# Placing a tile's weighted sum next to another tile's scores, and sharing a division between VectorE and GpSimd, in a cross-attention and expert kernel

## The chip, the cores and the metric

The kernel runs on one core of one Trainium2 chip. The metric is the device time in microseconds of one execution; lower is better. Three executions of the kernel before took 1203.09, 1205.06 and 1205.17 us, a median of 1205.06 us.

## What is computed

The input `x` has 32 sequences of 256 tokens with 256 features. Two layers follow each other, each with a residual and a scalar gate:

```python
x = x + tanh(g_xattn) * attention(layernorm(x), ctx, ctx)   # 16 heads, 77 keys, then @ W.T + b
x = x + tanh(g_ffn) * ffn(layernorm(x))

def attention(q, k, v):          # 16 heads of 16 features
    scores = q @ k.T / sqrt(16)
    scores = where(causal or padded, -inf, scores)
    return softmax(scores) @ v @ W.T + b

def ffn(x):                      # 2 groups of 4 experts, 2 experts per token
    shared = swiglu(x @ w_in.T) @ w_out.T
    h = swiglu(x @ w1.T)
    group = argmax(softmax(x @ wg.T + gb))
    p = softmax(x @ we.T + eb over the group's experts) * p_group
    a, b = the two largest of p
    return shared + p[a] * h @ w2[a].T + p[b] * h @ w2[b].T
```

Everything is float32.

## The kernel before

The 8192 tokens are cut into 16 blocks of 512, a block into 4 tiles of 128 tokens (t = 0 to 3); a tile fills the 128 partitions. Three things go on at once for different blocks.

The attention of a tile is a chain of small steps, each a function:

- `first_stats`, `normed`, `queries`: the layer norm of `x` on VectorE, and its transposition on TensorE (tile `pt`, copied by ScalarE into `qT`). `biased` adds the output bias to `x` on GpSimd (L338).
- `scores` (L353): 8 small matmuls, each over 32 rows of TensorE, into the PSUM tile `sc` of four banks. Its pool `ps_sc` has one buffer.
- `masked` (L366): VectorE adds the mask and moves the scores to SBUF (`ws`, two buffers in turn). `largest` (L378, L379): the maximum of each head and its scaling.
- `exps` (L387): ScalarE, one instruction for each head, with its sum. In block 0 half of the heads go another way: `shifted` (L396) on VectorE, `wide` (L410) on ScalarE, `summed` (L415) on VectorE.
- `divided` (L424, L425): VectorE takes the reciprocal of the sums and multiplies all 16 heads of 77 values in place.
- `transposed` (L440): ten transpositions into three banks `ptr`, which ScalarE copies into `aT` (L443).
- `weighted` (L465): the sum of values, small matmuls that each write 32 columns, into `vT`; ScalarE copies it into `oT`.
- `o_proj` (L485), `residual` (L502), `stats2`, `normed2`, `keep`: the output matmul `po`, the residual, the second layer norm and its transposition into `xT` (copied at L302).

The dense work of a block follows: `shared` (matmuls `ph`, L790, and `pys`, L842), `routed` (`pr`, L818), and the experts' matmuls `py` (L905) for 128 tokens of one pair of experts at a time. Those tokens are collected through DRAM: `rec` is written to `rows` by an indirect DMA from GpSimd (L859), and read back as `r_q` by SyncE's queue; `hp` (L898) transposes it, and GpSimd writes `out` (L925). Which pair a token takes is worked out by `logits` (`plT`), `choice`, `places` and `listing` on VectorE, in many short instructions.

The order is written out by hand. The dense work is a generator that pauses twice in each unit (after a unit's matmuls, and after their eviction); every other step has a place, counted in such units, and is issued when the counter reaches it. A block from number 5 on takes 28 units. The places stand in the table `PLACES`: one row for a step, whose first four numbers are for the tiles of block 0, the next four for blocks 1 to 4, the ninth for blocks 5 to 14, and the tenth for block 15. A tile's place is `s0 + t * gap` and the step's number on top; steps on TensorE come half a unit later. The engines then run their queues strictly in the order in which the steps were issued. All PSUM tiles but `sc` share one pool of four banks.

In blocks 5 to 14 `gap` is 7, `scores` is at -2 and `weighted` at 9.5. So `weighted` of a tile comes 2.5 units before `scores` of the tile two behind it, which are at -2 + 14.

Of the kernel before, what the change touches and what calls it, by code (L numbers as in the profile page):

```python
# [11 lines left out]
ALU = mybir.AluOpType  # L12
AX = mybir.AxisListType

P = 128
D = 256
NC_ = D // P
NH = 16
# [15 lines left out]
BB = 2  # L34
EPS = 1e-5
WIDE = 8
SURE = 22
AHEAD = 4
MASKED = -1.0e30
# [2 lines left out]
PLACES = {  # L42


    "s0": (12.5, 17, 20, 12.5, 17, 17, 18, 16, 16.5, 16.5),
    "gap": (3, 14.5, 3, 3.5, 3, 5, 4, 5.5, 7, 7),
    "stats": (-8, -8, -16, -13.5, -12, -11, -10.5, -9, -8.5, -9),
    "stats_gap": (0.25, 0, -3, -4.25, 0.75, 1.25, 1.25, 1.5, 0.75, 1),
    "bias": (-0.5, -1, -5.5, -8.5, -6, -1.5, -0.5, -1.5, -2.5, -2.5),
    "normed": (-4.5, -3, -5, -3, -3.5, -4.5, -3.5, -4, -4, -5),  # L50
    "normed_gap": (4, 2.75, 1.5, 3.75, 1, 2, 3.25, 1.75, 1.5, 1.75),
    "queries": (-2.5, -3, -5.5, -3.5, -4, -3, -3.5, -4, -3, -4.5),
    "queries_copy": (0, 0.5, -0.5, 3, 0.5, 0.75, 0, 0.75, 0, 1.75),
    "scores": (-2.5, -5, -1.5, -1, -2, -1, -1, 0, -2, -1.5),
    "masked": (0.5, -1.5, -0.5, 0.5, 0.5, 0, 0, 1, 1, 1),
    "largest": (1, 1, 2, 1, 2, 2, 1, 1.5, 2.5, 2.5),
    "exps": (3.5, 4.5, 5.5, 4.5, 3, 3, 2, 3, 3.5, 3),
    "exps_gap": (-1, -1.25, -0.75, -1.5, 0.5, 0.5, 0.5, 0.5, 0.75, 0.5),
    "divided": (5.2, 5.2, 6.2, 5.2, 5.7, 5.2, 4.2, 5.2, 6.7, 6.7),
    "transposed": (8.5, 8, 8, 7.75, 8, 6, 7.5, 7, 8.5, 8.5),  # L60
    "aT": (0.75, 0.5, 1.75, 0.75, 0.25, 0.25, 0, 0.25, 0.5, 0.25),
    "weighted": (9.5, 9.5, 10.5, 9.5, 10, 9, 8, 10, 9.5, 9.5),
    "oT": (0.25, 1.5, 0, 1, 0, 0.75, 1, 0, 0, 0),
    "o_proj": (12, 11, 12.5, 11, 10.5, 10.5, 10, 11, 10, 10),
    "residual": (13, 13, 13.5, 12.5, 11.5, 12, 11, 12, 11, 11),
    "stats2": (13.5, 13.5, 14.5, 13, 12.5, 13.5, 12.5, 13, 12, 12),
    "normed2": (16, 15, 15, 14.5, 14, 14.5, 13.5, 14, 13.5, 13),
    "keep": (16, 15.5, 15.5, 15.5, 14.5, 14.5, 16, 15, 14, 14),
    "xT": (1.25, 1.25, 2.25, 1, 0.25, 0.75, 0, 0, 0.5, 0.5),
    "logits": (10, 12, 15.5, 14.5, -1, -1, 0, -1, -1, -1),  # L70
    "lT": (0, -0.5, -1.25, -2.5, 0.25, 0, 0, 0, 0.25, 0),
    "choice": (11, 10.5, 17, 18.5, 0, 0, 0, -0.5, -0.5, -0.5),
    "choice1": (14, 9.5, 12, 15.5, 1, 1, 1, 0.5, 0.5, 1),
    "choice2": (12.5, 14.5, 10.5, 10.5, 7.5, 2.5, 1.5, 1, 1, 2),
    "choice3": (15.5, 13, 17.5, 14.5, 2, 8.5, 9.5, 2.5, 2.5, 4.5),
    "places": (15.5, 14, 20, 18.5, 3, 3.5, 3, 2, 2.5, 3),
    "places1": (16, 11.5, 11, 3, 4.5, 7, 4, 3.5, 8, 3.5),
    "places2": (16, 17.5, 24, 24.5, 9.5, 5.5, 8.5, 8.5, 4, 7.5),
    "listing": (5, 2, 0, 2.5, 19.5, 9.5, 7.5, 7, 5.5, 5),
    "listing_gap": (2.25, 5, 1.25, 3.75, 1.75, 2, 3, 4.25, 4.75, 4),  # L80
    "load": (-0.5, 2, -2, 0, -10, 9, 4.5, 6, 19.5, 6.5),
    "biased": (-2.5, -2.5, 0, 5, 7.5, 3.5, 5.5, 4.5, 3.5, 11),
    "biased_gap": (2.25, 2.25, 1.5, 2, 0.375, 1.25, 1.75, 2.75, 0.5, 1.25),
    "ends": (9.5, 13.5, 6.5, 11, 5, 10, 7, -3, 11, 6),
    "ends_gap": (2.5, 2, 0, -0.5, 2.25, -2.5, -1, 4.25, 0, 1.75),
    "context": (2, 5, 4, 6.5, -8, 4, -5.5, 0.5, 5.5, 5),
    "shifted": (2, 2, 3, 3.5, -2.5, -1.5, 4.5, -1.5, -5, -13),
    "wide": (4.6, 3.6, 4.1, 4.1, 4, 1.5, 0.5, -0.5, 9, 6),
    "summed": (4.9, 4.9, 4.4, 4.4, -1, 1, -2.5, -9, 5, 0.5),
}  # L90


# [1 line left out]
def kernel(  # L94
# [19 lines left out]
    nc = tc.nc  # L114
    NBLK, SK = mask.shape[0], mask.shape[2]
# [259 lines left out]
    def largest(s, t):  # L375
        i = s["i"]
        mx = p2.tile([P, NH], F32, tag="mx", name=f"mx_{i}_{t}")
        nc.vector.tensor_reduce(mx, s["ws", t], AX.X, ALU.max)  # L378
        nc.vector.tensor_scalar_mul(mx, mx, -(DH**-0.5))  # L379
        s["mx", t] = mx  # L380
        s["pr", t] = p2.tile([P, NH, SK], F32, tag="pr", name=f"pr_{i}_{t}")
        s["rc", t] = p2.tile([P, NH], F32, tag="rc", name=f"rc_{i}_{t}")
# [11 lines left out]
    def shifted(s, t):  # L394
        heads = slice(NH - WIDE, NH)
        nc.vector.scalar_tensor_tensor(  # L396
            s["pr", t][:, heads, :],
            s["mx", t][:, heads].unsqueeze(2).to_broadcast([P, WIDE, SK]),
            DH**0.5,
            s["ws", t][:, heads, :SK],  # L400
            ALU.mult,
            ALU.add,
        )
        s["exps", t] = s.get(("exps", t), 0) + WIDE
        s["shifted", t] = True

    def wide(s, t):
        assert s.pop(("shifted", t))
        pr = s["pr", t][:, NH - WIDE :, :]
        nc.scalar.activation(pr, pr, AF.Exp, scale=DH**-0.5)  # L410
        s["wide", t] = True

    def summed(s, t):
        assert s.pop(("wide", t))
        nc.vector.tensor_reduce(  # L415
            s["rc", t][:, NH - WIDE :], s["pr", t][:, NH - WIDE :, :], AX.X, ALU.add
        )
        s["summed", t] = True

    def divided(s, t):  # L420
        assert s["i"] or s.pop(("summed", t))
        pr, rc = s["pr", t], s.pop(("rc", t))
        assert s.pop(("exps", t)) == NH
        nc.vector.reciprocal(rc, rc)  # L424
        nc.vector.tensor_tensor(  # L425
            pr, pr, rc.unsqueeze(2).to_broadcast([P, NH, SK]), ALU.mult
        )

    def transposed(s, t):

# [554 lines left out]
    def at(place, fn, pe=False):  # L985
        events.append((place + 0.5 * pe, len(events), fn))
# [7 lines left out]
    def place(b, what, t=0):  # L994
        return PLACES[what][t if b == 0 else 3 + min(b, 5) + (b + 1 == NBLK)]

    def tile_events(b, t, e):
        def p(what):
            return e + place(b, what, t)
# [3 lines left out]
        at(p("largest"), lambda: largest(blocks[b], t))  # L1003
        for k in range(4 - 4 * WIDE // NH if b == 0 else 4):
            at(
# [3 lines left out]
        if b == 0:  # L1009
            at(p("shifted"), lambda: shifted(blocks[b], t))  # L1010
            at(p("wide"), lambda: wide(blocks[b], t))
            at(p("summed"), lambda: summed(blocks[b], t))
        at(p("divided"), lambda: divided(blocks[b], t))
        at(p("transposed"), lambda: transposed(blocks[b], t), pe=True)
        for k in range(3):
# [41 lines left out]
    for b in range(NBLK):  # L1057
        e = begins[b]
        gap = place(b, "gap")
        s0 = e - place(b, "s0") - (NT - 1) * gap  # L1060
# [39 lines left out]
    def finish(tiles):  # L1100
        gens = [pair_tile(k) for k in tiles]
        for g in gens[:AHEAD]:
            next(g)
        for g in gens[:2]:
            next(g)
            next(g)
        for _ in pair_tiles(gens):
            pass

    with tc.manual_schedule(  # L1110
# [16 lines left out]
        count = nc.values_load(counts[0], min_val=0, max_val=n_rest)  # L1127
        finish(rest[:SURE])
        with tc.If(count > SURE):
            finish(rest[SURE:])  # L1130

# [76 lines left out]
```

## Time and profile before

| What | us |
|---|---|
| median of three executions | 1205.06 |
| the profiled execution, whole | 1204.88 |
| its span, first to last instruction | 1203.1 |
| TensorE busy with matmuls | 1158.4 |
| VectorE busy | 898.4 |
| ScalarE busy | 615.1 |
| GpSimd busy | 291.6 |

The profile names the engines PE (TensorE's matmuls), PEld (its weight loads), DVE (VectorE), ACT (ScalarE), POOL (GpSimd) and SP (SyncE, which issues DMAs). A group's row gives the line, the engine, the operation, what is written from what, the sizes, the number of instructions and their busy and mean time. A row of the timeline gives the start in us from the span's start, the length in us, and the same names; a bracket at its end gives the idle time before it and what ended it. Matmuls on TensorE overlap, so the time of a group is best read from its start to the start of the next.

### The profile page before, as it was taken

To read this page: it belongs to the slowest core of one execution; us is meant where nothing else is said; L and a number is where in the kernel's file an instruction comes from. 1 tells how busy PE (TensorE), PEld (TensorE's weight loads), DVE (VectorE), ACT (ScalarE), POOL (GpSimd) and SP (SyncE) were. 2 spreads that over 40 slices of the span, in tenths; PEclk is the share of its full clock that TensorE was granted. 3 is DMA by queue.
4 is the path that set the end of the run, shared out by engine and by line. 5 is a ranking of instruction groups with operands and counts; after the bars stand their busy time and mean duration, and the time that the engine had idled before them with its cause. 6 is when DMAs were issued, how large, how long until landed. Compare 5 with 4: busy or idle time off the path is not lost.

```text
span 1203.1 us, 23398 instructions
## 1 busy us (share of the span) xinstructions
PE 1158.4 (96%) x7548; PEld 785.0 (65%) x7548; DVE 898.4 (75%) x2504; ACT 615.1 (51%) x2594; POOL 291.6 (24%) x509
## 2 busy tenths in 40 slices
PE   4799999999999999999999999999999999999997
PEld 3576555556575766767576676757667575757886
DVE  7988979897868688786868878686887868574222
ACT  3875675555555645555564555556455555411110
POOL 2013131222130312313031231302223122224222
PEclk9899999999999999999999999999999999999999
DMA  7102061213131121313112131311213020134442
GB/s 251 40 15 93 15 245 37 71 41 124 40 106 58 67 85 65 112 41 107 58 67 84 58 120 40 102 62 67 84 53 107 28 81 31 46 102 165 126 116 78
DMA packets 39016, 98.89 MB, mean 82 GB/s; under 512 B 6824, under 2 KB 17962, under 8 KB 38384
## 3 DMA queue, kind: packets, MB, share of 16 engines
q1 hardware_dynamic: 28976, 60.78, 16.5%
q0 software_dynamic: 9488, 36.47, 7.7%
q8 instruction: 64, 1.05, 0.4%
q14 instruction: 56, 0.46, 0.1%
q10 hardware_dynamic: 432, 0.13, 0.0%
HBM read 60.50 MB, written 39.74 MB: 83 GB/s over the span
## 4 chain that ended last, share of the span: by engine, by line
PE 69%; issue 6%; POOL 2%; ACT 2%; DVE 1%; POOLq 0%; DVEq 0%; ACTq 0%
PE pr L818 15%; PE py_q L905 15%; PE ph L790 14%; PE pys L842 7%; PE vT L465 4%; PE po L485 3%; PE ptr L440 3%; PE sc L353 3%; POOL out L925 2%; PE pt L299 2%; PE hp_q L898 2%; ACT hT_q L900 1%; PE plT L529 1%; ACT sa L802 1%; ACT aT L443 0%
## 5 line engine op out<-in xcount | busy, mean ns | idle before, releaser
L387 ACT ACTIVATE pr<-ws,mx 128x77 f32<-128x77 f32 x992 | 341.3, 349 | 10.5 <-DVE mx L379 10.0
L790 PE MATMUL ph<-xT,win_sb 128*128 128x512 f32 (+1 forms) x544 | 242.4, 581 | 1.8 <-ACT xT L302 1.0
L818 PE MATMUL pr<-w_sb,xT 128*128 128x512 f32 x512 | 243.1, 603 | 0.7 <-DVE rec L833 0.3
L905 PE MATMUL py_q<-w_sb,hT_q 128*128 x784 | 184.8, 382 | 4.3 <-ACT hT_q L900 4.3
L387 ACT ACTIVATION_READ_ACCUMULATOR pr<-ws,mx 128x1 f32 x992 | 188.9, 190 | 0.0
L905 PEld LDWEIGHTS py_q<-w_sb,hT_q 128*128 128x128 f32 x784 | 143.5, 190 | 25.7 <-ACT hT_q L900 7.4
L790 PEld LDWEIGHTS ph<-xT,win_sb 128*128 128x128 f32 x544 | 97.6, 191 | 87.3 <-issue 72.9
L818 PEld LDWEIGHTS pr<-w_sb,xT 128*128 128x128 f32 x512 | 90.5, 190 | 84.9 <-issue 74.1
L285 POOL TENSOR_TENSOR rs_f<-ve_f,nhalf 128x1 f32<-128x1 f32 x64 | 36.7, 573 | 380.3 <-DVE ve_f L283 356.4
L443 ACT COPY aT<-ptr 124x512 f32<-124x512 f32 (+1 forms) x192 | 86.8, 523 | 71.0 <-PE ptr L440 70.8
L842 PE MATMUL pys<-wout_sb,gT 128*128 128x256 f32 x512 | 121.7, 380 | 0.0
L859 POOL DMA_INDIRECT rows<-rec,posi x64 | 69.2, 1081 | 204.0 <-DVE rec L856 85.6
L842 PEld LDWEIGHTS pys<-wout_sb,gT 128*128 128x128 f32 x512 | 95.6, 190 | 26.0 <-issue 12.6
L925 POOL DMA_INDIRECT out<-acc_q,r_q x49 | 61.5, 1255 | 146.8 <-DVE acc_q L916 120.8
L425 DVE TENSOR_TENSOR pr<-pr,rc 128x1232 f32<-128x1232 f32 x64 | 92.9, 1452 | 2.2
L366 DVE TENSOR_TENSOR ws<-sc,mb 128x1232 f32<-128x1232 f32 x64 | 91.6, 1432 | 2.0 <-PE sc L353 2.0
L378 DVE TENSOR_REDUCE mx<-ws 128x16 f32<-128x1248 f32 x64 | 92.5, 1445 | 0.5
L440 PE MATMUL ptr<-ident,pr 128*124 128x128 f32 x640 | 83.6, 277 | 2.9 <-DVE sr L832 1.1
L440 PEld LDWEIGHTS ptr<-ident,pr 128*124 128x124 f32 x640 | 73.2, 141 | 19.2 <-issue 6.2
L302 ACT COPY xT<-pt 128x256 f32<-128x256 f32 x64 | 23.8, 371 | 116.8 <-PE pt L299 116.8
L905 PE MATMUL py_last<-w_sb,hT_last 128*128 x352 | 79.6, 379 | 0.3 <-ACT hT_last L900 0.3
L828 ACT ACTIVATE sr<-pr 128x512 f32<-128x512 f32 x64 | 38.0, 593 | 78.1 <-PE pr L818 63.6
(181 smaller groups left out, 1577.8 us busy)
## 6 DMA issues: line engine op xcount, KB each, us to landing
r_q<-rows SPq DMA_DIRECT2D x49, 386.0 KB
va<-in_vd SPq DMA_DIRECT2D x16, 640.0 KB
r_last<-rows SPq DMA_DIRECT2D x22, 386.0 KB
x<-in_x SPq DMA_DIRECT2D x64, 128.0 KB
kbd<-in_kbd SPq DMA_DIRECT2D x16, 308.0 KB
w_sb<-in_w2T SPq DMA_DIRECT2D x4, 1024.0 KB
mi<-in_mask SPq DMA_DIRECT2D x16, 77.0 KB
win_sb<-in_w_inT SPq DMA_DIRECT2D x1, 1024.0 KB
```

The lines of the kernel that those rows point to most:

```text
L366: nc.vector.tensor_tensor(ws[:, :, :SK].rearrange("p (g h) k -> p g h k", g=RG), s.pop(("sc", t))[:, :, : NC_ * PK].rearrange("p g (h k) - ...
L378: nc.vector.tensor_reduce(mx, s["ws", t], AX.X, ALU.max)
L387: nc.scalar.activation(s["pr", t][:, h, :], s["ws", t][:, h, :SK], AF.Exp, bias=s["mx", t][:, h : h + 1], scale=DH**-0.5, accum_out=s["rc" ...
L425: nc.vector.tensor_tensor(pr, pr, rc.unsqueeze(2).to_broadcast([P, NH, SK]), ALU.mult)
L440: nc.tensor.transpose(pt[:CR, (r - r0) * P : (r - r0 + 1) * P], pr[:, row : row + CR], ident)
L443: s["aTc", t, r0 // 4] = lambda r0=r0, n=n, pt=pt: nc.scalar.copy(aT[:, r0 : r0 + n, :].rearrange("k r q -> k (r q)"), pt[:CR, : n * P])
L790: nc.tensor.matmul(ab[half][:, : n * P], lhsT=win_sb[:, c, f0 : f0 + P], rhs=s["xT"][:, c, cols], start=(c == 0), stop=(c == NC_ - 1),)
L818: nc.tensor.matmul(ab[half], lhsT=s["xT"][:, c, t * P : (t + 1) * P], rhs=w1_sb[:, c, half * HID : (half + 1) * HID], start=(c == 0), stop ...
L842: nc.tensor.matmul(py[:, :D], lhsT=s["g"][:, m, t * P : (t + 1) * P], rhs=wout_sb[:, m, :], start=(m == 0), stop=(m == NM - 1),)
L859: put(nc.gpsimd.indirect_dma_start(out=rows, out_offset=bass.IndirectOffsetOnAxis(ap=s["pos"][:, t, :], axis=0), in_=rec, in_offset=None,), i)
L905: nc.tensor.matmul(py[:, j * D : (j + 1) * D], lhsT=hT[:, m, :], rhs=w2_sb[:, m, bass.ds(e_at[j], D)], start=(m == 0), stop=(m == NM - 1),)
L925: done_with(nc.gpsimd.indirect_dma_start(out=out, out_offset=bass.IndirectOffsetOnAxis(ap=ids, axis=0), in_=acc, in_offset=None, bounds_ch ...
```

## The change

Three things are changed.

First, in blocks 5 to 14 the places of `scores` go from -2 to -4.5. With a gap of 7, `scores` of tile t + 2 then comes at 9.5, where `weighted` of tile t stands too, directly ahead of it. In block 15 `scores` goes to -2 and `weighted` stays at 9.5, with the same gap of 7.

Second, the other places are set anew, in all blocks. In blocks 5 to 14 `masked` goes from 1 to 2 and `largest` from 2.5 to 2, `o_proj` from 10 to 11.5 and `residual` from 11 to 12; the loads of `x` come 5 units earlier. In block 0 the second `queries` come ahead of the second `scores`.

Third, in blocks 0 and 1 (`SHARED = 2`) the multiplication of `divided` is split: heads 0 to 7 on VectorE, heads 8 to 15 on GpSimd.

```diff
+SHARED = 2
...
-    "s0": (12.5, 17, 20, 12.5, 17, 17, 18, 16, 16.5, 16.5),
-    "gap": (3, 14.5, 3, 3.5, 3, 5, 4, 5.5, 7, 7),
+    "s0": (12.5, 14, 21, 14.5, 17, 17, 18, 16, 16.5, 16.5),
+    "gap": (3, 4, 3, 2, 3, 5, 4, 5.5, 7, 7),
...
-    "scores": (-2.5, -5, -1.5, -1, -2, -1, -1, 0, -2, -1.5),
-    "masked": (0.5, -1.5, -0.5, 0.5, 0.5, 0, 0, 1, 1, 1),
-    "largest": (1, 1, 2, 1, 2, 2, 1, 1.5, 2.5, 2.5),
-    "exps": (3.5, 4.5, 5.5, 4.5, 3, 3, 2, 3, 3.5, 3),
+    "scores": (-2.5, -2.5, -1.5, 0, -2.5, -1.5, -1.5, 0, -4.5, -2),
+    "masked": (1, -1.5, -1, 0.5, 0.5, 0, 0, 1, 2, 2),
+    "largest": (1, 1.5, 2, 1.5, 2, 2, 1, 1.5, 2, 2.5),
+    "exps": (3.5, 4.5, 5.5, 4.5, 3, 3, 2, 3, 4, 4),
...
-    "weighted": (9.5, 9.5, 10.5, 9.5, 10, 9, 8, 10, 9.5, 9.5),
+    "weighted": (9, 9, 10, 9, 10, 9, 8.5, 9.5, 9.5, 9.5),
...
-    "o_proj": (12, 11, 12.5, 11, 10.5, 10.5, 10, 11, 10, 10),
-    "residual": (13, 13, 13.5, 12.5, 11.5, 12, 11, 12, 11, 11),
+    "o_proj": (12, 11, 11.5, 10.5, 11, 10.5, 10, 11, 11.5, 10),
+    "residual": (13, 13, 13.5, 12, 11.5, 12, 11, 12, 12, 11),
...
-    "load": (-0.5, 2, -2, 0, -10, 9, 4.5, 6, 19.5, 6.5),
+    "load": (4, 11.5, -1.5, -2, -0.5, 18.5, 17, 8, 24.5, 7),
...
         nc.vector.reciprocal(rc, rc)
-        nc.vector.tensor_tensor(
-            pr, pr, rc.unsqueeze(2).to_broadcast([P, NH, SK]), ALU.mult
-        )
+
+        parts_ = [(nc.vector, 0, NH)]
+        if s["i"] < SHARED:
+            parts_ = [(nc.vector, 0, NH // 2), (nc.gpsimd, NH // 2, NH)]
+        for engine, h0, h1 in parts_:
+            engine.tensor_tensor(
+                pr[:, h0:h1], pr[:, h0:h1],
+                rc[:, h0:h1].unsqueeze(2).to_broadcast([P, h1 - h0, SK]), ALU.mult,
+            )
```

## The prediction

> **What bounds the kernel now.** I read the page's busy shares first, then its slices, then busy time by stage, then TensorE's waits in the stage where it idles.
>
> ```profile
> PE 1158.4 (96%) x7548; PEld 785.0 (65%) x7548; DVE 898.4 (75%) x2504; ACT 615.1 (51%) x2594; POOL 291.6 (24%) x509
> PE   4799999999999999999999999999999999999997
> ```
>
> TensorE is busy for 96% of the span and below nine tenths only in the first two slices and the last. The stages (start:end, span, then busy time of PE, PEld, DVE, ACT, POOL, granted clock, DMA share, GB/s) make that sharper:
>
> ```profile
> 10.00:50.00 40.00, 25.02 (x304) 18.82 (x296) 38.97 (x72) 25.21 (x107) 4.12 (x6) 0.96 0.45 147
> 50.00:60.00 10.00, 7.71 (x39) 5.71 (x40) 7.78 (x18) 8.83 (x50) 0.87 (x3) 0.83 0.32 111
> 300.00:1050.00 750.00, 746.38 (x4895) 498.38 (x4895) 586.00 (x1641) 409.40 (x1738) 177.37 (x309) 1.00 0.21 71
> ```
>
> From 300 to 1050 us TensorE has 3.6 us of holes: there only a shorter TensorE stream shortens the kernel. From 10 to 50 us VectorE is busy 38.97 of 40 us and TensorE waits for it:
>
> ```profile
> PE sc L353 <- DVE ws L366: 10.0, 3, 7.0
> PE pt L299 <- DVE xn L290: 7.2, 1, 7.2
> PE pt L299 <- ACT aT L443: 3.7, 1, 3.7
> ```
>
> (waiter, what it waited for, us in all, times, longest.) So the change has two separate parts: the middle is TensorE's stream, the start VectorE's queue.
>
> **Part 1: `weighted` next to `scores`.** TensorE's timeline, one tile of the steady middle:
>
> ```profile
> 603.26 1.98 PE L818 MATMUL pr<-w_sb,xT 128*128 128x512 f32 x4
> 605.17 1.08 PE L465 MATMUL vT<-aT,va 124*32 124x128 f32 x32
> 606.18 1.98 PE L818 MATMUL pr<-w_sb,xT 128*128 128x512 f32 x4
> 608.00 1.03 PE L485 MATMUL po<-wo_sb,oT 128*128 128x256 f32 x4
> ...
> 611.03 1.88 PE L818 MATMUL pr<-w_sb,xT 128*128 128x512 f32 x4
> 612.84 0.81 PE L353 MATMUL sc<-kbd,qT 32*128 32x154 f32 x16
> 613.58 0.66 PE L299 MATMUL pt<-ident,xn 128*128 128x128 f32 x4
> 614.07 1.88 PE L818 MATMUL pr<-w_sb,xT 128*128 128x512 f32 x4
> 615.79 1.89 PE L842 MATMUL pys<-wout_sb,gT 128*128 128x256 f32 x8
> ```
>
> Read start to start, since matmuls overlap. Four pr matmuls between full-array neighbours take 615.79 - 614.07 = 1.72. Before `sc` they take 612.84 - 611.03 = 1.81: entering a small-tile group costs 0.09. After `vT` they take 608.00 - 606.18 = 1.82: leaving costs 0.10 (0.06 when transposes follow: four pt take 0.49 after `sc`, 0.44 else, in the same view). Before `vT` they take 1.91. `vT` itself takes 1.01, `sc` 0.74.
>
> A rule speaks against a gain: the Trainium skill, "TensorEngine Tiling (Array Packing)", Key Properties, says that changing the tiling mode, not merely the tile, drains TensorE. `vT` tiles columns (124*32) and `sc` rows (32*128), so side by side they still change mode. The trace of before has such a pair:
>
> ```profile
> 259.54 1.08 PE L465 MATMUL vT<-aT,va 124*32 124x128 f32 x32
> 260.55 0.81 PE L353 MATMUL sc<-kbd,qT 32*128 32x154 f32 x16
> 261.28 0.66 PE L299 MATMUL pt<-ident,xn 128*128 128x128 f32 x4
> ```
>
> `vT` 1.01, `sc` 0.73: nothing is added between them. By the row a pairing saves one entry and one exit, by the rule only about one of them. I take the row.
>
> Count from the built order of TensorE's instructions: runs of small-tile groups (`sc`, `vT`, `plT`) fall from 135 to 98; 40 `sc` stand directly behind a `vT`, against 5. Pricing every boundary of both orders by the class it falls in (entry 0.09 from a full group, 0.19 from ph or pr into `vT`, 0 from transposes; exit 0.10, or 0.06 into transposes) gives 24.7 us before and 17.8 after: **-6.9 us**. By the rule it would be about -3.4. The matmuls are otherwise the same in number and shape.
>
> Does a new wait eat it? `ps_sc` has one buffer, so `scores` of tile t+1 must wait for `masked` of t. Before, `masked` ends 7.9 to 11.8 us ahead of the next `sc` in steady blocks. After, `masked` stands later, `scores` earlier. The tightest case (t = 1): VectorE after the last py of the block does the two acc (0.48 each), then ws (1.43), about 2.5 us with 0.15 to wake; TensorE has plT 0.58, ptr 1.15, ph 1.72, pl 0.20, vT 1.01 = 4.66 before `sc`. Slack 2.1 us. For t = 2 the orders match before's, where ws ends at 658.24 and vT at 659.88: 1.6. A second tight place is `pt` of tile 0's `normed2`: its VectorE queue starts 0.6 us later than before (acc and `masked` now precede `largest`), where before had 653.69 - 652.75 = 0.9 in hand; 0.1 to 0.3 is left after part 1 shortens TensorE. Nothing is lost if these hold; I allow 0 to 0.3 us per block, up to 3 us in all, as width.
>
> `o_proj` and `residual` move later by 1.5 and 1 steps; `keep` stays, with 5 us of full-array matmuls between po and pt to hide residual 0.48, statistics 0.6 + 0.15, pow 0.57 and xn 0.41. On SP, the load of x now stands ahead of the block's first `r_q` load, not behind its last: it waits for an x freed some 8 steps earlier, and `r_q` is used twelve units (over 20 us) later. No cost.
>
> **Part 2: the halves of the division in blocks 0 and 1.** VectorE saves half of 1.44, 0.72, in each of 8 tiles, if GpSimd's half runs beside it. The trace speaks against that:
>
> ```profile
> 214.41 1.45 DVE L425 TENSOR_TENSOR pr<-pr,rc 128x1232 f32<-128x1232 f32 x1
> 214.43 2.01 POOL L338 TENSOR_TENSOR x<-x,bo 128x256 f32<-128x256 f32 x1
> ...
> 156.16 0.74 POOL L338 TENSOR_TENSOR x<-x,bo 128x256 f32<-128x256 f32 x1
> 156.41 1.79 DVE L425 TENSOR_TENSOR pr<-pr,rc 128x1232 f32<-128x1232 f32 x1
> ```
>
> An addition of 0.72 alone takes 2.01 behind a division, and a division of 1.44 takes 1.79 behind an addition: whoever comes second waits until the first is done. "SBUF — State Buffer", Who interferes with whom, says the same and for which: VectorE with two SBUF inputs or in a two-port mode excludes GpSimd's reads. VectorE's half comes first (it waits for nothing), GpSimd's follows; then VectorE's next instruction counts. In block 0 that is `shifted` (mx and ws, both SBUF) for tiles 0 to 2 and `normed2` for tile 3 (a TENSOR_SCALAR; one like it took 0.90 for 0.41 beside GpSimd): all blocked until GpSimd ends. No row has 128x616 on GpSimd; from 0.72 at 256, scaled fully, 1.73; with 0.2 fixed (its 2-element copy), 1.45. I take 1.6.
>
> So a tile in block 0 costs VectorE 0.72 + 1.6 = 2.3 for 1.44: four times +0.9 = 3.5 us. Following the new queue by hand from 10 us adds 1.8: tile 1's division cannot start before 28 us, as half its exps now stand behind the three aT copies on ScalarE, and `largest` 2 and two statistics moved ahead. `normed2` of tile 1 starts near 50.8 rather than 45.50. Were the halves side by side it would start near 44.6.
>
> The end of this stage is the first shared matmul:
>
> ```profile
> 52.34 0.36 ACT L302 COPY xT<-pt 128x256 f32<-128x256 f32 x1
> 52.75 3.60 PE L790 MATMUL ph<-xT,win_sb 128*128 128x256 f32 x8 [0.51 <-ACT xT L302]
> ```
>
> Before, that xT copy stands behind all 16 exps of block 1's first tile and starts 6.8 us after their `largest` ends (45.59). In the new order only 8 stand ahead: 8 x 0.345 = 2.8, then xT 0.4, oT 0.4, po 1.1: 4.7. So ph starts at 45.59 + 5.2 + 4.7 = 55.4: **+2.7 us**; side by side 45.6 - 0.9 + 4.7 = 49.3, -3.4. In block 1 two tiles' halves are followed by PSUM-fed evictions, which the lock spares (-0.7 each), one by a bias with two SBUF inputs (+0.9), one by statistics (-0.3): together -0.8 on VectorE, off TensorE's path by then, counted 0. From 60 to 300 us TensorE idles 7.8 us, in small waits that the moved steps reshuffle; I keep their sum, with 3 us either way. The half-clock window (0.83 in 50:60) may fall elsewhere: 1.7 either way.
>
> **Sum.** -6.9 + 2.7 = -4.2 on a span of 1203.1 (execution 1204.88; median shown 1205.06, within the runs' spread of it). 1205.06 - 4.2 = 1200.8.
>
> **Cases.**
> - A, forecast, 0.48: pairing pays in full, the halves run in turn: 1200.8; its own range 1198 to 1203.
> - B, 0.30: the wait hits VectorE where it would have waited for ScalarE anyway, or moved steps fill TensorE's start. For it: the xT copy comes earlier, ScalarE is 25 of 40 us busy. Against: 38.97 of 40 on VectorE. -6.9 - 3.4: 1194.8.
> - C, slower, 0.12: `scores` waits for `masked` through the one buffer, once or more per block from 5 on. Price: excess over the slack, times 11 blocks. It cancels the saving above 0.4 us per block and shows as slower from 0.6; at 1 us, 1200.8 + 11 = 1212. For it: `masked` now stands behind the block's last acc with 2.1 us left instead of 10.8. Against: VectorE idles 22% of the middle.
> - D, 0.10: the change doesn't do what it says: the mode change between `vT` and `sc` costs one drain (-3.4), and the start is late: -0.7, 1204.4.
>
> About 0.2%, 2.4 us, can be told from no change. Faster: A but for its edge, B: 0.74. Same: D and A's edge: 0.14. Slower: 0.12. Range 1193.5 to 1206 leaves out C's bulk and B's lower edge.
>
> **What would show it.** Right: in the middle pr takes 1.82 only behind `sc`, `sc` follows `vT` at 1.01, and the period from one block's first `sc` to the next falls from 70.34 by about 0.7. GpSimd's half takes about 2.3 us including its wait, `shifted` 2.4 instead of 0.79; ph starts near 55. Wrong: a row "sc waits for ws" after 300 us; a ph before 51.

## The result, and the profile after

The changed kernel took 1208.02 us in the median of 17 executions (1204.51 to 1212.28), the kernel before 1204.94 in 17 (1202.20 to 1205.95). The ratio is 1.0033, with a 95% interval of 1.0025 to 1.0041: **slower by a third of a percent**, where 1200.8 was forecast. The profiled execution took 1209.44 us, its span 1207.6.

The busy shares and TensorE's slices of the page:

```profile
PE 1159.6 (96%) x7548; PEld 788.3 (65%) x7548; DVE 903.7 (75%) x2504; ACT 616.4 (51%) x2594; POOL 316.2 (26%) x517
PE   4799999999999999999999999999999999998997
```

TensorE does as many matmuls as before, for nearly as long. New is an 8 in the slices near 1090 us. Busy time by stage (columns as in the prediction), of after:

```profile
10.00:50.00 40.00, 26.12 (x276) 19.69 (x276) 39.15 (x64) 24.37 (x101) 12.54 (x12) 0.87 0.45 146
50.00:60.00 10.00, 7.52 (x57) 5.61 (x56) 8.91 (x24) 9.76 (x56) 3.53 (x4) 0.94 0.38 118
300.00:1050.00 750.00, 743.19 (x4896) 499.49 (x4895) 589.83 (x1636) 410.00 (x1738) 190.22 (x309) 1.00 0.21 71
1050.00:1116.00 66.00, 62.30 (x238) 40.20 (x236) 36.17 (x125) 8.83 (x19) 23.77 (x35) 0.95 0.36 120
```

and of before, the stage that the prediction left out:

```profile
1050.00:1112.00 62.00, 60.64 (x244) 40.38 (x243) 36.89 (x127) 9.85 (x19) 24.73 (x36) 1.00 0.36 128
```

Both last rows end within 2 us behind the last expert matmul on an `r_q` (done at 1110.2 and 1114.8). In before TensorE lacks 1.4 us there, in after 3.7, and the clock is 0.95 instead of 1.00. In the middle TensorE's holes grew from 3.6 to 6.8 us: a shorter stream with more waits in it. At the start (0 to 60 us) TensorE's waits changed hands:

```profile
PE pt L300 <- DVE xn L291: 8.1, 3, 6.6
PE ptr L447 <- DVE pr L431: 5.5, 2, 3.9
PE sc L354 <- DVE ws L367: 3.0, 3, 1.7
```

Where do the 4.6 us between the two spans (1203.08 and 1207.65) come from? The first `pys` of each block serves as a mark in both timelines. After minus before: -1.19 us at block 5, -1.17 at block 15, and +4.57 at the last matmul. So the start is 1.2 ahead, the ten blocks with the pairing gain **nothing** (693.10 us before, 693.12 after), and the end loses **5.7**. Most of the ten gain 0.1 to 0.3; two of them together lose 0.4 and one loses 0.6.

**The middle.** TensorE in one steady block of after, around tile 2:

```profile
668.65 1.89 PE L849 MATMUL pys<-wout_sb,gT 128*128 128x256 f32 x8
670.44 0.78 PE L300 MATMUL pt<-ident,xn 128*128 128x128 f32 x4
671.27 1.65 PE L447 MATMUL ptr<-ident,pr 128*124 128x128 f32 x10
672.76 1.88 PE L825 MATMUL pr<-w_sb,xT 128*128 128x512 f32 x4
674.57 1.08 PE L472 MATMUL vT<-aT,va 124*32 124x128 f32 x32
675.58 0.81 PE L354 MATMUL sc<-kbd,qT 32*128 32x154 f32 x16
676.32 1.98 PE L825 MATMUL pr<-w_sb,xT 128*128 128x512 f32 x4
```

The pairing is there: `vT` takes 1.01 to the start of `sc`, `sc` 0.74, nothing between them. But four `pt`, worth 0.44, take 0.83, and `ptr` 1.49 (672.76 - 671.27), where before it took 1.28:

```profile
601.98 1.25 PE L440 MATMUL ptr<-ident,pr 128*124 128x128 f32 x10
603.26 1.98 PE L818 MATMUL pr<-w_sb,xT 128*128 128x512 f32 x4
```

VectorE and GpSimd of after at the same time:

```profile
666.82 0.17 DVE L284 TENSOR_SCALAR ve_a<-st 128x4 f32<-128x4 f32 x1
...
667.49 1.44 DVE L431 TENSOR_TENSOR pr<-pr,rc 128x1232 f32<-128x1232 f32 x1
669.89 0.74 DVE L291 TENSOR_SCALAR xn<-x,st,rs_a 128x256 f32<-128x256 f32 x2 [0.95 <-POOL rs_a L286]
670.54 0.68 DVE L839 SCALAR_TENSOR_TENSOR sr<-sr,pr 128x512 f32<-128x512 f32 x1
671.31 0.69 DVE L840 TENSOR_TENSOR rec<-sr,pr 128x512 f32<-128x512 f32 x1
```

```profile
666.56 1.05 POOL L866 DMA_INDIRECT rows<-rec,posi  x1 [0.81 <-DVE bn L278]
667.64 2.21 POOL L286 TENSOR_TENSOR rs_a<-ve_a,nhalf 128x4 f32<-128x4 f32 x1
```

Read from below. The power for the next block's layer norm (`rs_a`, the variance to the power of -0.5) can start at 666.99, when VectorE has written `ve_a`, but GpSimd is still issuing the write of a record. It begins at 667.64, just behind VectorE's division, and ends 0.92 after that division does: 2.21 us for what takes 1.02 where nothing stands in its way, as early in the same trace:

```profile
29.99 1.02 POOL L286 TENSOR_TENSOR rs_a<-ve_a,nhalf 128x4 f32<-128x4 f32 x1 [1.49 <-DVE ve_a L284]
```

VectorE's `xn` waits 0.95 us for it, and behind `xn` stand `sr` and `rec`, which empty the two banks of `pr`. `ptr` needs such a bank: `sr` ends at 671.22, `ptr` begins at 671.27. So a wait on VectorE for GpSimd shows on TensorE as a late transposition. It recurs: VectorE waits for `rs_a` 9 times, 8.6 us, between 300 and 1050 us, against once, 0.8 us, in before.

**The end.** The last block of after, TensorE first, then VectorE, then ScalarE:

```profile
1079.99 1.89 PE L849 MATMUL pys<-wout_sb,gT 128*128 128x256 f32 x8
1081.72 3.60 PE L825 MATMUL pr<-w_sb,xT 128*128 128x512 f32 x8
1085.15 1.89 PE L849 MATMUL pys<-wout_sb,gT 128*128 128x256 f32 x8
1090.15 6.76 PE L825 MATMUL pr<-w_sb,xT 128*128 128x512 f32 x8 [3.11 <-DVE rec L863]
```

```profile
1083.61 0.48 DVE L749 SCALAR_TENSOR_TENSOR at_last<-slot,skip_last 128x312 f32<-128x312 f32 x1
1089.61 0.48 DVE L863 SCALAR_TENSOR_TENSOR rec<-pys,tgf,x 128x256 f32<-128x256 f32 x1 [5.52 <-remote]
```

```profile
1089.67 0.60 ACT L835 ACTIVATE sr<-pr 128x512 f32<-128x512 f32 x1 [10.60 <-remote]
```

VectorE waits for `pys` of tile 1, whose matmuls were done at 1081.9, and ScalarE for the half of `pr` done at 1083.6. Both start only at 1089.6. The trace's semaphore records say why: TensorE's signals came late, and VectorE and ScalarE went on 0.02 us behind them.

```
TensorE's group, and its end     its semaphore counts up     late by
pr, tile 1, second half 1080.15            1082.42             2.3
pys, tile 1             1081.88            1089.59             7.7
pr, tile 2, first half  1083.60            1089.65             6.1
pr, tile 2, second half 1085.31            1089.71             4.4
pys, tile 2             1087.04            1089.80             2.8
```

In the same stretch (1081.7 to 1089.5) SyncE's steps mostly follow each other at 0.70 us or twice that, where the median of the whole trace is 0.20. TensorE then has no free bank and stands for 3.1 us, and its clock falls: the granted clock is half for 6.8 us from 1089.5, so that the next `pr` takes 6.76 instead of 3.60. (6.8 us is two of the windows of some 3.4 us in which, by the Trainium skill, "TensorE: Matmul & The Clock Gate", Part 1, the clock is judged; the half-clock stretches within all traces here are 3.4, 6.8 or 10.2 us long.) The wait and the slow clock, 3.1 and 3.2 us, cover the 5.7. What GpSimd does at that time is a run of twelve writes:

```profile
1082.59 0.98 POOL L703 DMA_INDIRECT rows<-none,toi_end  x1 [0.30 <-issue]
1083.88 1.07 POOL L703 DMA_INDIRECT rows<-none,toi_end  x1 [0.30 <-issue]
1085.25 0.98 POOL L703 DMA_INDIRECT rows<-none,toi_end  x1 [0.30 <-issue]
1086.21 0.23 POOL L857 COPY rec<-wab 128x2 f32<-128x2 f32 x1
```

These are `ends`: they fill the rest of each pair's table with empty records, three to a step, and the change moved them from place 6, with 1.75 units from step to step, to 5.5 with 0.75. In before the first record's write stands behind the sixth; in after all twelve stand ahead of it.

### The profile page after: what moved, and what is told of

Same layout as the page of the kernel before. It is cut to its first block, busy times and chain, and to the rows that moved or that the text cites. A ratio compares the mean times of both kernels' runs of the same rounds, so it can differ in the third digit from the quotient of the medians.

```text
span 1207.6 us, 23417 instructions
## 1 busy us (share of the span) xinstructions
PE 1159.6 (96%) x7548; PEld 788.3 (65%) x7548; DVE 903.7 (75%) x2504; ACT 616.4 (51%) x2594; POOL 316.2 (26%) x517
## 4 chain that ended last, share of the span: by engine, by line
PE 67%; issue 6%; POOL 2%; ACT 2%; DVE 1%; another core or an unknown queue 0%; POOLq 0%; ACTq 0%
PE py_q L912 14%; PE ph L797 14%; PE pr L825 14%; PE pys L849 7%; PE vT L472 4%; PE po L492 3%; PE ptr L447 3%; PE sc L354 3%; PE pt L300 2%; POOL out L932 2%; PE hp_q L905 1%; ACT hT_q L907 1%; DVE rec L840 1%; PE plT L536 1%; ACT aT L450 0%
## 5 line engine op out<-in xcount | busy, mean ns | idle before, releaser
L912 PE MATMUL py_q<-w_sb,hT_q 128*128 x784 | 180.7, 381 | 3.6 <-ACT hT_q L907 3.6
L825 PEld LDWEIGHTS pr<-w_sb,xT 128*128 128x128 f32 x512 | 93.7, 192 | 93.3 <-issue 83.1
L447 PE MATMUL ptr<-ident,pr 128*124 128x128 f32 x640 | 87.1, 281 | 9.4 <-DVE pr L431 5.5
L923 DVE SCALAR_TENSOR_TENSOR acc_q<-py_q,r_q 128x256 f32<-128x256 f32 x49 | 23.7, 484 | 88.7 <-PE py_q L912 88.3
L431 DVE TENSOR_TENSOR pr<-pr,rc 128x1232 f32<-128x1232 f32 (+1 forms) x64 | 88.1, 1376 | 2.2
L472 PEld LDWEIGHTS vT<-aT,va 124*32 124x32 f32 x2048 | 52.5, 110 | 35.8 <-issue 25.8
```

The lines of the kernel that those rows point to most:

```text
L431: engine.tensor_tensor(pr[:, h0:h1], pr[:, h0:h1], rc[:, h0:h1].unsqueeze(2).to_broadcast([P, h1 - h0, SK]), ALU.mult,)
L447: nc.tensor.transpose(pt[:CR, (r - r0) * P : (r - r0 + 1) * P], pr[:, row : row + CR], ident)
L472: nc.tensor.matmul(vT[q * PR * DH : (q + 1) * PR * DH, w * P : (w + 1) * P], lhsT=s["va"][:CR, b, w, k, at : at + PR, :].rearrange("p a d ...
L825: nc.tensor.matmul(ab[half], lhsT=s["xT"][:, c, t * P : (t + 1) * P], rhs=w1_sb[:, c, half * HID : (half + 1) * HID], start=(c == 0), stop ...
L912: nc.tensor.matmul(py[:, j * D : (j + 1) * D], lhsT=hT[:, m, :], rhs=w2_sb[:, m, bass.ds(e_at[j], D)], start=(m == 0), stop=(m == NM - 1),)
```

## The experiments

Each series (a, b, c, d) ran on a chip of its own, beside runs of before. "Period" is the median time from one steady block's first `sc` to the next (70.35 in before, 70.23 in after). With the stall, VectorE's longest wait in the last block is 3.7 to 6.3 us and TensorE's (the "hole" of the expectations) 2.4 to 3.1; without it they are at most 1.9 and 1.0.

| Kernel | us | ratio to before, 95% | period | stall at the end |
|---|---|---|---|---|
| a1_ends | 1202.90 | 0.9997 (0.9986 to 1.0007) | 70.23 | no |
| a2_stats | 1196.98 | 0.9934 (0.9920 to 0.9948) | 69.38 | no |
| a3_noshare | 1202.64 | 0.9994 (0.9985 to 1.0003) | 70.23 | no |
| a4_middle | 1204.02 | 1.0000 (0.9991 to 1.0009) | 70.24 | no |
| b1_after | 1208.32 | 1.0028 (1.0013 to 1.0044) | 70.23 | yes |
| b2_share | 1204.36 | 1.0000 (0.9991 to 1.0009) | 70.35 | no |
| b3_unpaired | 1208.32 | 1.0033 (1.0021 to 1.0045) | 70.10 | yes |
| b4_best | 1195.85 | 0.9930 (0.9917 to 0.9944) | 69.39 | no |
| c1_ends | 1202.80 | 0.9993 (0.9984 to 1.0001) | 70.23 | no |
| c2_ends_late | 1206.80 | 1.0025 (1.0015 to 1.0036) | 70.24 | yes |
| c3_noshare | 1207.48 | 1.0035 (1.0022 to 1.0048) | 70.23 | yes |
| c4_start_before | 1197.90 | 0.9948 (0.9935 to 0.9960) | 69.39 | no |
| d1_spread | 1202.98 | 0.9991 (0.9982 to 1.0000) | 70.24 | no |
| d2_before_dense | 1209.18 | 1.0045 (1.0031 to 1.0058) | 70.34 | yes |

### The end: a1_ends, c1_ends, b1_after, c3_noshare

```diff
-    "ends": (..., 5.5),
-    "ends_gap": (..., 0.75),
+    "ends": (..., 6),
+    "ends_gap": (..., 1.75),
```

a1_ends: 

> After, with the two numbers of the last block's end-of-table scatters (ends, ends_gap) set back to before's 6 and 1.75. Theory E (the end's loss is an order of DMAs): in after 9 of the 12 scatters are issued ahead of the block's r_q loads, so the loads wait for them and go out at 1081.7 to 1091.2 us in the middle of the scatters, and in just that time TensorE's semaphore updates land up to 5 us late, VectorE and ScalarE stand still, TensorE waits 3.1 us and its clock drops. With before's numbers only 3 scatters stand ahead of the loads: no late update, no hole near 1090, last block like before's. Time 1208.0 - 4.6 = 1203.4, and the runs lie within 4 us of each other instead of 8. Rival F (something else in the last block's new places, or a late instruction fetch, makes the stall): 1207 to 1208.5, the hole stays.

It came out as theory E said. But so did a3_noshare, which leaves `ends` where after has it:

```diff
-SHARED = 2
+SHARED = 0
```

a3_noshare: 

> After, with the division of blocks 0 and 1 on VectorE alone (SHARED = 0). Theory L (the halves run in turn under a lock): in after VectorE takes 2.45 us for half a division and the blocked shifted, against 2.07 for the whole division and shifted before; so without sharing VectorE is 0.3 to 0.4 us per tile quicker in block 0, the first ph comes at about 51 instead of 52.0, and the time is 0 to 1.2 us lower: 1207.4. Rival S (the halves overlap enough to pay): first ph later than 52.5 and 0.5 to 3 us slower, 1208.5 to 1211.

1202.64 instead of 1207.4, and no hole: on that chip no kernel had one, not even a2_stats and a3_noshare with after's `ends`, so a1_ends had shown nothing of `ends`. Hence after again, unchanged:

b1_after: 

> After, unchanged, beside this series' runs of before. Every kernel of the first series ended without the stall, also two that left the last block's places as they were, so the order of scatters and loads alone doesn't decide it. Theory G (the stall belongs to the program of after, an alignment of the last block's DMAs with the rest that a shift of 1 to 5 us undoes): 1207 to 1209 again, a hole near 1090 and late updates again. Rival H (the stall came with the circumstances of those executions, not with the program): no hole, about 1202.5 to 1203.5, within 0.1% of before, and the change is then worth what a1_ends showed, nothing.

The hole is back to a tenth of a microsecond (VectorE resumes at 1089.6 again), so it is no accident of one execution, as rival H had it; but the chip counts too, since the first series' chip never shows it. The third series then set the two kernels side by side.

c1_ends: 

> The same kernel as a1_ends (after with before's numbers for the last block's scatters), again, since the first series showed no stall in any kernel and the second showed it in each whose r_q loads stand behind scatters (b1_after, b3_unpaired) and in none whose loads stand ahead (b2_share, b4_best). Theory E: no hole near 1090, no late updates, 1202.5 to 1203.5. If the circumstances decide alone, c1_ends and c3_noshare end alike.

c3_noshare: 

> The same kernel as a3_noshare (after without the shared division, its scatters where after has them), again. Theory E: where the stall shows at all, it shows here: a hole near 1089, 1206 to 1208, 0.5 to 1 below after because the first ph comes 0.9 us earlier. If sharing had anything to do with the stall: no hole, 1202.6 as in the first series.

1202.80 without a hole, 1207.48 with one: the places of `ends` decide, and sharing has no part in it. The first series stays the exception, on its chip alone. (In fact six of the twelve writes stand ahead of the loads in after and none in before, not nine and three, as the first text says.)

### Which property of ends: c2_ends_late, d1_spread, d2_before_dense

Two things changed together: the loads of `r_q` stand behind six of the writes, and the twelve follow each other without the first record's write between them.

```diff
-    "ends": (..., 5.5),
+    "ends": (..., 7),
```

c2_ends_late: 

> After, with the last block's scatters 1.5 units later (ends 7 for 5.5), their spacing of 0.75 kept: all twelve then stand behind the four r_q loads in the order of issue (in after six stand ahead), but follow each other as densely as in after. Theory E in its narrow form (what matters is that loads wait for scatters and are issued among them): no hole, 1202.5 to 1203.5. Rival D (what matters is that the scatters are dense): the stall stays, 1206 to 1209.

Theory E in that form fell: with all loads ahead, 1206.8, and TensorE's signals late again (VectorE takes up `pys` of tile 1 1.6 us after its end, that of tile 2 5.0 after). So the opposite:

```diff
-    "ends_gap": (..., 0.75),
+    "ends_gap": (..., 1.75),
```

d1_spread: 

> After, with the spacing of the last block's scatters alone as before (ends_gap 1.75 for 0.75, ends left at 5.5). Three scatters then still stand ahead of the r_q loads, so the loads still wait for scatters and go out among them, but the write of the block's first record stands between the sixth and the seventh scatter instead of behind all twelve. If the loads among scatters make the stall: a hole again, 1206 to 1209. If the unbroken run of twelve scatters makes it (as c2_ends_late suggests): no hole, 1202.5 to 1203.5.

1202.98 and no hole, although the four loads went out at 1079.4 to 1085.4, among the writes. GpSimd's timeline of d1_spread:

```profile
1080.03 0.98 POOL L703 DMA_INDIRECT rows<-none,toi_end  x1 [0.31 <-issue]
1081.00 0.50 POOL L857 COPY rec<-wab 128x2 f32<-128x2 f32 x1
1081.45 0.18 POOL L858 COPY rec<-tok 128x1 int32<-128x1 int32 x1
1081.57 0.09 POOL L862 MEMSET rec<- 128x1 f32 x1
1082.64 0.99 POOL L866 DMA_INDIRECT rows<-rec,posi  x1 [0.97 <-POOL rec L862]
1083.93 1.21 POOL L703 DMA_INDIRECT rows<-none,toi_end  x1 [0.30 <-issue]
1086.30 0.99 POOL L703 DMA_INDIRECT rows<-none,toi_end  x1 [1.16 <-issue]
```

Six writes, then a pause of 1.6 us with the record's three small instructions in it, one record, one write, another pause of 1.2. The loads also go out earlier than in after (1081.7 to 1090.8), but c2_ends_late had them earlier still and stalled. Whether the record or the pauses matter was not separated. SyncE's steps are at 0.70 us here too, from 1080.0 to 1082.1 and once at 1084.7, yet no signal of TensorE's comes late. Last, the two numbers of after in the kernel before, with nothing else of the change:

d2_before_dense: 

> Before, with after's two numbers for the last block's scatters alone (ends 5.5, ends_gap 0.75); all else, the middle, the start and the division, as before. If these two numbers carry the loss at the end by themselves: the hole appears in a kernel that has nothing else of the change, +4 to +6 against before, 1208 to 1210. If it needs the rest of the change: within 1 us of before.

1209.18, +5.1 us: they carry the loss by themselves, without anything that the change does to blocks 5 to 14. TensorE in d2_before_dense; it waits behind the last `pys` of the block, where before has no such wait:

```profile
1091.08 1.89 PE L842 MATMUL pys<-wout_sb,gT 128*128 128x256 f32 x8
1094.30 0.66 PE L898 MATMUL hp_q<-ident,r_q 128*128 128x128 f32 x4 [1.33 <-DVE rec L856]
1097.41 1.11 PE L898 MATMUL hp_q<-ident,r_q 128*128 128x128 f32 x4 [2.45 <-DVE sr L832]
```

### The middle: a2_stats, b3_unpaired, a4_middle

```diff
-    "stats": (..., -11, -11),
+    "stats": (..., -12, -11),
```

a2_stats: 

> After, with the first statistics of blocks 5 to 14 one unit earlier (-12 for -11), nothing else. Theory P (the pairing's gain is given back by a wait on VectorE): in after the four statistics end 1.5 units ahead of the first layer norm, GpSimd's power of 4 values takes 2.2 us behind a scatter, VectorE's xn waits 0.95 us for it, the evictions behind it (sr, rec) come late, their bank isn't free, and TensorE's ptr starts 0.4 us late and pr another 0.2. With the statistics a unit earlier the power is done in time: period of a steady block 70.23 -> about 69.6, ten blocks, 1208.0 - 6 = 1202 (the end stays as in after). Rival B (four banks are too few for pt, ptr and pys between two pr, whatever VectorE does): period 70.2, time 1207 to 1208.5.

The period fell to 69.38, by 0.85, a little more than expected, and VectorE's waits for `rs_a` are gone: the power now stands ahead of the record and of the division (at 664.68) and takes 1.14. (The time fell by 11, since this series had no hole at the end.) TensorE of a2_stats at the same place:

```profile
668.90 0.60 PE L300 MATMUL pt<-ident,xn 128*128 128x128 f32 x4
669.33 1.25 PE L447 MATMUL ptr<-ident,pr 128*124 128x128 f32 x10
670.42 1.88 PE L825 MATMUL pr<-w_sb,xT 128*128 128x512 f32 x4
```

`pt` takes 0.43 again and `ptr` 1.09: the banks were never too few, they were emptied late. Then from this version the pairing alone is taken away:

```diff
-    "scores": (..., -4.5, -2),
+    "scores": (..., -2, -2),
```

b3_unpaired: 

> The version with earlier statistics (a2_stats, 1197.0), with scores of blocks 5 to 14 back at -2, so that no weighted stands next to a scores there, all else the same. Theory P: the pairing itself is worth what the boundaries were priced at, 0.65 to 0.75 us per block, so the steady period rises from 69.4 to about 70.1 and the time to 1197.0 + 7 = 1204. Rival N (the gain of a2_stats came from the statistics alone and the pairing is worth nothing, as by the rule on modes at most half): 1197 to 1200.5.

The period is 70.10: **the pairing is worth 0.72 us per block** (from the first `pys` of block 5 to that of block 15, 692.5 us against 686.0: 6.5 in ten). The time, 1208.3 instead of 1204, also holds the hole at the end, which a2_stats did not have; only the period is to be compared. So the period of after can be taken apart: 70.35 before, -0.25 by the column's other places (with the earlier statistics), -0.72 by the pairing, +0.85 by the wait for the power, 70.23.

The whole ninth column alone, in before:

a4_middle: 

> Before, with after's ninth column of places alone (blocks 5 to 14: the pairing and what was placed anew around it); start, end and division as before. Theory P with E: the steady period falls from 70.35 to about 70.2 only (pairing -0.73, wait for the power +0.63), the end stays undisturbed: 1205.0 - 1.2 = 1203.8. Rival C (the end's stall hangs on what blocks 5 to 14 leave behind, not on the last block's own places): 1207 to 1208. If the recorded prediction's sum held for the middle alone it would be 1198.

1204.02, a ratio of 1.0000: what the middle's new places gain and lose cancels. (It ran on the chip without the stall, so of the end it says nothing.)

### The shared division: b2_share

```diff
+SHARED = 2
...
-        nc.vector.tensor_tensor(
-            pr, pr, rc.unsqueeze(2).to_broadcast([P, NH, SK]), ALU.mult
-        )
+        parts_ = [(nc.vector, 0, NH)]
+        if s["i"] < SHARED:
+            parts_ = [(nc.vector, 0, NH // 2), (nc.gpsimd, NH // 2, NH)]
+        for engine, h0, h1 in parts_:
+            ...
```

b2_share: 

> Before, with the shared division alone (blocks 0 and 1), all places as before. Theory L: in block 0 each half on VectorE and the blocked instruction behind it take 0.3 to 0.4 us more than the whole division and that instruction did, four times on VectorE's queue; first ph at about 53.5 instead of 52.75, time +0.5 to +1.5: 1204.3 to 1205.3 against 1203.8 of before. By the recorded estimate of 1.6 for GpSimd's half it would be +3.5 for VectorE and about +2.7 for the time: 1206.5. Rival S (the overlap pays): 1202 to 1203.

1204.36, ratio 1.0000, first `ph` at 52.62 against 52.75, where 53.5 was expected: neither gain nor loss beyond the interval. The reverse, after without sharing, agrees: 1202.64 (a3_noshare) beside 1202.90 (a1_ends) on the same chip. Still the two halves do not run side by side. VectorE and GpSimd in after, tile 1 of block 0:

```profile
26.62 0.80 DVE L431 TENSOR_TENSOR pr<-pr,rc 128x616 f32<-128x616 f32 x1
27.34 1.81 DVE L397 SCALAR_TENSOR_TENSOR pr<-mx,ws 128x616 f32<-128x616 f32 x1
29.07 0.41 DVE L278 BATCH_NORM_STATS2 bn<-x 128x6 f32<-128x256 f32 x1
```

```profile
26.66 1.83 POOL L431 TENSOR_TENSOR pr<-pr,rc 128x616 f32<-128x616 f32 x1 [4.75 <-DVE rc L425]
```

GpSimd's half starts with VectorE's and ends at 28.49; VectorE's half ends at 27.42. So, if the halves take turns, GpSimd needed 1.07 for itself; and `shifted`, 0.79 alone, took 1.81, until 0.66 after GpSimd's end. From the division to what follows `shifted` VectorE spends 29.07 - 26.62 = 2.45, before 29.68 - 27.61 = 2.07: +0.38 for a tile.

### What beats both: b4_best, c4_start_before

b4_best is after with the earlier statistics, `SHARED = 0` and before's `ends`. c4_start_before is before with after's ninth column and the earlier statistics in it.

b4_best: 

> After, with three edits: the first statistics of blocks 5 to 14 a unit earlier, the division of blocks 0 and 1 on VectorE alone, the last block's scatters at before's places. If the gains add (period 69.4 in ten blocks as in a2_stats, start as in a3_noshare, no stall at the end): 1202.6 - 8.5 = 1194, 0.8% faster than before. If the earlier statistics disturb the start as they seemed to in a2_stats (2.5 us later at block 1): 1196.5.

c4_start_before: 

> Before, with after's ninth column and the statistics a unit earlier in it; start, blocks 1 to 4, last block and division as before. Against a4_middle (1204.0) the power's wait is gone: ten blocks by 0.85, 1204.0 - 8.5 = 1195.5, the same as b4_best with another start. If before's start is worth something against after's (its granted clock is higher, 0.997 against 0.991 to 0.995): 1193.5 to 1194.5.

1195.85 and 1197.90, 0.70% and 0.52% faster than before. b4_best lies between its two expectations: the period is the expected 69.39 and the ten blocks gain 7.2 us on before, but block 1's first `pys` comes 3.6 us after that of before, and TensorE runs at half clock for 20 us of its first 133, against 7 in the trace of before. c4_start_before misses by 2.4: it starts as before does, but loses 3.2 us from the first `pys` of block 2 to that of block 3 (a4_middle 2.4), where the ninth column's steps meet the blocks ahead of them. That was not followed further.

## Why the prediction was wrong

**The pairing, right.** Entries and exits of small-tile groups were priced at 6.9 us in all, about 0.7 per block; measured 0.72 per block. The row (`vT` 1.01, `sc` 0.73, nothing between) held, and half the gain, which the prediction took from the rule on tiling modes, is excluded: `sc` follows `vT` at 1.01 and takes 0.74 in all steady blocks of after.

**"Does a new wait eat it?", wrong: this is the step that failed in the middle.** It looked at two places, `sc` behind `ws` and `pt` of tile 0 behind `normed2`, and allowed 0 to 0.3 us per block. Both held: after 300 us `sc` never waits for `ws`, and `pt` waits for `xn` once, 1.2 us. (`masked` of tile 1 was done 2.2 us ahead of the next `sc`, as worked out, that of tile 2 1.1 us and not 1.6.) The wait that came was on neither path. The diff moves the layer norm of the next block with `scores` (`normed` from -4 to -6.5), and its statistics too, but by a little less: from the last statistics to the first `xn` there were 2.25 units, after it 1.5.

```diff
-    "stats": (..., -8.5, -9),
-    "stats_gap": (..., 0.75, 1),
-    "normed": (..., -4, -5),
+    "stats": (..., -11, -11),
+    "stats_gap": (..., 1, 1),
+    "normed": (..., -6.5, -5),
```

I had not followed that chain, VectorE to GpSimd and back, nor asked what is queued behind `xn`: the evictions that free TensorE's banks. The prediction put this chain at nothing; it cost 0.85 us per block, more than the 0.72 that the pairing brought. In kind it is rival C, a wait in place of the one removed, but at another place, so C's own sign (`sc` waiting for `ws`) never showed.

**The sum, wrong: it had no term for the last block.** Block 15's column was not followed; its `ends` lines are not spoken of at all. Following GpSimd's queue through block 15 would have shown that the twelve writes now stand ahead of the first record's. That gives their order, not the 5 us: before has no run of more than six, and none of its rows shows a signal of TensorE's held up. It was an unknown cost that belonged on the slow side of the range.

**The halves of the division, right in kind, too dear.** `shifted` is held up, and side by side (case B) is excluded. But GpSimd's half takes 1.07 by itself, not 1.6, so a tile costs VectorE +0.38 and not +0.9; 1.81 was seen for `shifted` where 2.4 was forecast, and 1.83 for GpSimd's half where 2.3 was.

**The first `ph`, wrong.** 55.4 was forecast, +2.7; it came at 52.02. Besides the halves, the 1.8 that I got by following VectorE's new queue by hand is refuted: tile 1's division started at 26.36, not after 28, and its `normed2` at 46.77, not near 50.8. The earlier xT copy that counted for case B did come. The start is even with before's, within the shifts of the half-clock stretches (10.2 and 3.4 us in after, 3.4 and 3.4 in before). The sum had a slip besides: 3.5 + 1.8 is 5.3 and not 5.2, and the sum comes to 55.6, not 55.4.

**60 to 300 us, right** to within its allowance of 3: the lead over before is 0.5 us at block 0 and 1.2 at block 5 (between them it swings from 0.7 behind to 1.2 ahead).

Taken together: forecast -6.9 in the middle and +2.7 at the start; measured 0 in the middle, -1.2 at the start, +5.7 at the end of the profiled pair.

## What to carry to other kernels

When a step is moved, move its whole chain, and measure the slack of each link on every engine that it crosses: a wait of 0.95 us on VectorE for a small power on GpSimd took more than a saving on TensorE gave, because evictions stood behind it. Read the last stage of a kernel like any other, DMA issue by DMA issue, since nothing comes after it to make up for a stall. And price a change from two versions that differ in that change alone: the pairing was worth 7 us all along, and two other numbers of the same table hid it.

## What the runs showed of the hardware

Twelve indirect writes issued by GpSimd one after another, 1.28 us apart, with no other work between them, delayed TensorE's semaphores, by up to 7.7 us, from about the eighth write on. With one record's write after the sixth, and the pauses that came with it, none was late. Where a series has a kernel with and one without the stall, it cost 4.0 to 5.1 us (c2_ends_late and c3_noshare against c1_ends; d2_before_dense against before). It showed in the result, b1_after and b3_unpaired too, but not in a2_stats and a3_noshare, which ran with the same run of writes on one other chip.

SyncE's steps of 0.70 us go with it: in the result, b1_after, b3_unpaired, c3_noshare and d2_before_dense they last as long as the stall, in d1_spread they come for 2 us without one, and in a2_stats and a3_noshare they don't come. Why an unbroken run does it is open. One rival stands untested, the recording itself. The records of DMAs landing are incomplete, 5173 to 5276 of them, in the traces from the chips of the later series and in the first two, stall or not, but 5516 to 5520 in those from the chip without the stall. Every time on record comes with a recorded span and clock, so none here shows how these kernels run unrecorded.

GpSimd's power of four values a partition takes 1.02 us when nothing is in its way, and 2.21 when VectorE divides at the same time: the turns that VectorE and GpSimd take, which part 2 was about, also decided part 1.
